# Convolution and expert products of 512 columns in place of 256, in a deformable-convolution, attention and mixture-of-experts kernel

## The chip, the cores and the metric

The kernel runs on one core of a Trainium2 chip. The metric is the device time of one execution in microseconds (us); the median of three executions of the kernel before is 7870.18 us. A core has five engines that this document speaks of: TensorE (PE in the profile; its weight loads are listed apart as PEld), VectorE (DVE), ScalarE (ACT), GpSimd (POOL) and SyncE (SP), the last of which issues most of the DMA transfers here. Each engine runs its instructions in the order in which they were issued to it, and engines wait for each other through semaphores.

## The reference

The input is `x` of shape (4, 128, 64, 64): four images of 128 channels and 4096 positions. Two layers follow each other:

```python
# layer 0
x = x + deform_conv(_gn(x), ...)       # group norm, then a deformable 3x3 convolution
# layer 1, on tokens (4, 4096, 128)
t = _to_tokens(x)
t = t + attn(_ln_t(t), ...)
t = t + experts(_ln_t(t), ...)
```

- The deformable convolution first computes offsets and masks with a 3x3 convolution (27 outputs), gathers four neighbours of each of the nine taps, blends them with bilinear weights times the mask into `samples` (channels x 9 taps x positions), and ends with `einsum('bckhw,ock->bohw', samples, w_flat)`: nine products of a 128x128 weight with the samples of a tap, summed.
- The attention has 16 heads of 8 dimensions over 4096 tokens. Queries, keys and values are the same array, so the score matrix before the softmax is symmetric. A small feed-forward network of 512 hidden units follows.
- The mixture of experts has 8 experts of 128x128. `einsum('bnd,edc->bnec', x, expert_w)` is computed for all eight, the two best by the router are weighted and summed.

All arithmetic is in fp32.

## The kernel before, in words

**The attention loop is the backbone.** For each image, for each of four groups of four heads (`g`) and each chunk of 512 queries (`sc`), a *run* goes through 32 tiles of 128 keys. One tile is one *step*; there are 3700 steps in all. A step has three parts:

- `scores` (line 1147): four fp32r matmuls of 128 keys x 512 queries, one for each head, into two PSUM tiles `sc` of [128, 2, 512], and one exponential over each `sc` tile on ScalarE (line 1164), whose result `e` goes to SBUF. The `sc` tiles come from a pool of three; the `e` tiles from a ring of six.
- the *fill*: at most one piece of other TensorE work, described below.
- `context` (line 1168): four fp32 matmuls that multiply `e` with the values, side by side in four strips of 32 output columns, summed over the run in one PSUM bank `acc`.

The main loop (line 1307) issues the scores of step n+2 (`LAG = 2`), then lets the planner place a fill (line 1335), then issues the context of step n (line 1365). So TensorE's order is: scores of n+2, fill, context of n, scores of n+3, and so on. A fp32 matmul shows in the trace as two records (two passes), an fp32r one as one.

In some runs part of the score matrix is taken from an earlier run by symmetry: VectorE transposes the `e` tiles (`turn`, line 1046), they go to DRAM and come back (`et`), and `from_turned` (line 1096) multiplies them, also as fills.

**All else is done beside it.** Generators produce the other work and yield, ahead of each piece, what it needs of TensorE and VectorE:

- `prepare(b)` (line 762) makes image b ready: group norm, a table of corners in DRAM, offsets (`om_ps`), gathers by GpSimd (line 575), the blend on VectorE (lines 589 to 601), the samples out to DRAM and back as `sT`, and `convolved` (line 633) with the convolution products, then `features`, which yields keys, queries and values. Image 0 is prepared partly ahead of the loop and partly beside its first runs (the *opening*, the first 160 steps), image b+1 during the runs of image b.
- `finish(b, ch)` (line 989) takes a finished chunk of 512 tokens through the output projection (`ao_ps`), the feed-forward network (`h_ps`, `f_ps`) and `experts` (line 882). At the end of the loop what is left is drained.

**The planner `Beside`** (line 62) decides at build time when each piece goes in. It keeps a modelled clock that a step moves on by `STEP = 1.82`, and a TensorE credit that grows by `RATE = 0.44` in a step, is capped at 0.44, and is lowered by a piece's cost `pe`; a piece may start if the credit after it is not under `-LATE = -0.50` (lines 136 and 143). In the opening the growth is 1.0 in a step, with the same cap (line 1299). All fills but those of `from_turned` write to one PSUM bank, `misc` (line 265). A piece that yields `hold=True` locks that bank until its last part has been issued; after that the bank counts as taken until VectorE's modelled read of it ends (lines 122 to 130).

**The two places that the change touches** use `by_columns` (line 270), which issues a product as four matmuls of 32 output columns, one for each strip. In `convolved` (lines 652 to 663) each of the nine taps is two products of 256 columns, `hf` 0 and 1, into the two halves of the bank: 18 pieces for a chunk of 512 positions, 576 in all, with the lock held over all 18. In `experts` (lines 958 to 980), for each of four blocks of 128 tokens and each half of the experts (`hf`), two products of 256 columns (two experts each) fill the bank, and VectorE then reads the 512 columns and multiplies them with the gates (line 970): 16 products of 256 columns for a chunk, 512 in all. Each piece asks for `MM256 = 0.44`, exactly the credit of a step.

Of the kernel before, what the change touches and what calls it, by code (L numbers as in the profile page):

```python
# [22 lines left out]
P = 128  # L23
# [7 lines left out]
KK = 9  # L31
# [162 lines left out]
FREE = -1.0  # L194


def need(pe=0.0, dve=0.0, lat=0.0, hold=False, after=0.0):

    return pe, dve, lat, hold, after


def ve(n, ops=1):

    return ops * (0.17 + n / 960.0)


MM256 = 0.44
MM128 = 0.23  # L210


def tr(n):

    return 0.13 + 0.115 * n
# [3 lines left out]
def kernel(  # L219
# [45 lines left out]
    def misc(name):  # L265
        if alone:
            return ps_s.tile([P, 2, 512], F32, tag="sc", name=name)[:, 0, :]
        return ps_m.tile([P, 512], F32, tag="misc", name=name)

    def by_columns(dst, lhsT, rhs, start, stop):  # L270

        for c in range(0, P, 32):
            nc.tensor.matmul(  # L273
                dst[c : c + 32], lhsT=lhsT[:, c : c + 32], rhs=rhs, start=start, stop=stop
            )
# [7 lines left out]
    def load(ap, shape, name):  # L283
        t = cpool.tile(shape, F32, name=name)
        nc.scalar.dma_start(out=t, in_=ap)
        return t
# [30 lines left out]
    wconv_sb = load(wconv, [P, KK, C], "wconv_sb")  # L317
# [14 lines left out]
    ew_sb = load(ew, [P, NE, C], "ew_sb")  # L332
# [150 lines left out]
    def offsets(b, xn, idx, wt):  # L483
# [3 lines left out]
        for half in range(2):  # L487
# [7 lines left out]
            for n, k in enumerate((4, 0, 1, 2, 3, 5, 6, 7, 8)):  # L495
                for top in range(0, 8, 4):
                    last = n == KK - 1 and top == 4
                    yield need(pe=MM256, dve=ve(512) if last else 0.0, lat=0.2 if last else FREE, hold=not last)
                    if n == 0 and top == 0:
# [63 lines left out]
    def deform(b, tab, idx, wt):  # L563
# [19 lines left out]
        for n, (ch, kg, j) in enumerate(units):  # L583
# [37 lines left out]
            if kg == 2:  # L621

                while featuring:
                    yield need(lat=1.0)
                featuring.append(True)
                beside.later(
                    beside.dve + 0.1,
                    lambda ch=ch: beside.add("prepare", convolved(b, ch), 0.5, True),
                )
# [3 lines left out]
    def convolved(b, ch):  # L633

        xr = work.tile([P, CH], F32, tag="p2", name=f"xr{b}_{ch}", bufs=NP2)
        nc.sync.dma_start(out=xr, in_=xf[b, :, CH * ch : CH * (ch + 1)])
        yield need(lat=2.5)

        sT = big.tile([P, KK, CH], F32, tag="xs", name=f"sT{b}_{ch}")

        def get(kg):
            for c in range(4):
                nc.sync.dma_start(
                    out=sT[32 * c : 32 * (c + 1), 3 * kg : 3 * kg + 3],
                    in_=smd[ch % 2][:, 3 * kg : 3 * kg + 3, c].rearrange("i k o n -> i k (o n)"),
                )

        get(0)
        yield need(lat=6.0)
        get(1)  # L650
        yield need(lat=4.0)
        for k in range(KK):
            if k == 2:
                get(2)
            for hf in range(2):
                last = k == KK - 1 and hf == 1
                yield need(pe=MM256, dve=ve(128, 4) if last else 0.0, lat=0.2 if last else FREE, hold=not last)
                if k == 0 and hf == 0:
                    po = misc(f"conv_ps{b}_{ch}")
                by_columns(  # L660
                    po[:, 256 * hf : 256 * (hf + 1)], wconv_sb[:, k, :],
                    sT[:, k, 256 * hf : 256 * (hf + 1)], k == 0 and hf == 0, last,
                )
        for o in range(4):
            of_block = xr.rearrange("p (j o t) -> p j o t", o=4, t=32)[:, :, o]
            nc.vector.scalar_tensor_tensor(
                of_block, po[:, P * o : P * (o + 1)].rearrange("p (j t) -> p j t", t=32), bconv_sb,
                of_block, ALU.add, ALU.add,
            )
        yield need(pe=tr(4), dve=ve(512))  # L670
        pt = misc(f"x2_ps{b}_{ch}")
        for k in range(4):
            nc.tensor.transpose(pt[:, P * k : P * (k + 1)], xr[:, P * k : P * (k + 1)], ident)
        x2 = work.tile([P, 4, C], F32, tag="p2", name=f"x2_{b}_{ch}", bufs=NP2)
        nc.vector.tensor_copy(x2, pt.rearrange("p (i c) -> p i c", c=C))
        beside.later(beside.dve, lambda: nc.sync.dma_start(out=x2d[b][ch], in_=x2))
        mean = work.tile([P, 4], F32, tag="lt_m", name=f"mean{b}_{ch}")
        rstd = work.tile([P, 4], F32, tag="lt_r", name=f"rstd{b}_{ch}")
        yield from features(b, ch, x2, mean, rstd)
# [107 lines left out]
    def temp2(name, shape=(P, 4, C)):  # L787
        return work.tile(list(shape), F32, tag="f2", name=name, bufs=NF2)
# [93 lines left out]
    def experts(b, ch, x4):  # L882
# [9 lines left out]
        uT = got.pop()  # L892
# [65 lines left out]
        for i in range(4):  # L958
            ws = [temp2(f"eo{b}_{ch}_{i}_{hf}") for hf in range(2)]
            for hf in range(2):  # L960
                for part in range(2):
                    yield need(pe=MM256, dve=ve(512) if part else 0.0, lat=FREE, hold=not part)
                    if part == 0:
                        pe = misc(f"e_ps{b}_{ch}_{i}_{hf}")
                    e0 = 4 * hf + 2 * part
                    by_columns(
                        pe[:, 256 * part : 256 * (part + 1)], uT[:, P * i : P * (i + 1)],
                        ew_sb[:, e0 : e0 + 2, :].rearrange("p e c -> p (e c)"), True, True,
                    )
                nc.vector.tensor_tensor(  # L970
                    ws[hf], pe.rearrange("p (e c) -> p e c", c=C),
                    gt[:, i, 4 * hf : 4 * (hf + 1), None].to_broadcast([P, 4, C]), ALU.mult,
                )
            yield need(dve=ve(512))
            w = ws[0]
            nc.vector.tensor_tensor(w, w, ws[1], ALU.add)
            yield need(dve=ve(256) + ve(128, 2), lat=0.2)
            nc.vector.tensor_tensor(w[:, :2, :], w[:, :2, :], w[:, 2:4, :], ALU.add)
            nc.vector.tensor_tensor(w[:, 0, :], w[:, 0, :], w[:, 1, :], ALU.add)
            nc.vector.tensor_tensor(x4[:, i, :], x4[:, i, :], w[:, 0, :], ALU.add)  # L980
# [8 lines left out]
    def finish(b, ch):  # L989
        x4 = temp2(f"x4_{b}_{ch}")  # L990
        nc.sync.dma_start(out=x4, in_=x2d[b][ch])

        rows = atd[b][ch].rearrange("g (h d) n -> (g h) d n", d=32)
        aT = temp2(f"aT{b}_{ch}", (P, CH))
        nc.sync.dma_start(out=aT, in_=rows[:, :HD])
        rd = work.tile([P, CH // HD], F32, tag="rd", name=f"rd{b}_{ch}")
        nc.sync.dma_start(out=rd, in_=rows[:, HD].rearrange("h (q n) -> h q n", q=HD))
        r = temp2(f"r{b}_{ch}")
        nc.sync.dma_start(out=r, in_=xtd[b][ch])
        yield need(lat=4.0)  # L1000
        yield need(dve=0.6, lat=0.1)
        nc.vector.reciprocal(rd, rd)
        yield need(lat=3.5)
        nc.sync.dma_start(out=rdd[b][ch].rearrange("h q n -> (h q) n"), in_=rd)
        yield need(lat=6.0)
        a4 = temp2(f"a4_{b}_{ch}")
        nc.sync.dma_start(
            out=a4.rearrange("p i c -> p (i c)"),
            in_=rdd[b][ch].rearrange("h q n -> h (q n)")[:, None, :].to_broadcast([HEADS, HD, CH]),
        )  # L1010
        yield from attention_out(b, ch, r, aT, a4)
        yield from feed_forward(b, ch, x4, a4)
        yield from experts(b, ch, x4)
# [82 lines left out]
    def from_turned(run, acc):  # L1096
# [3 lines left out]
        for kt in range(4):  # L1100
# [3 lines left out]
            for half in range(2):  # L1104
                yield need(pe=MM256, hold=None, after=landed)
                for t in (2 * half, 2 * half + 1):
# [135 lines left out]
    for n, (run, t) in enumerate(steps):  # L1242
        b, g, sc = runs[run][:3]
# [56 lines left out]
    with tc.manual_schedule(engines={PE, DVE, SP, POOL}):  # L1300
# [6 lines left out]
        while n < len(steps):  # L1307
# [11 lines left out]
            b, g, sc, ts, kind = runs[run]  # L1319
# [136 lines left out]
```

## Time and profile before

| | |
|---|---|
| median of 3 executions | 7870.18 us (7869.32 to 7878.19) |
| the profiled execution | 7908.98 us, its span 7907.1 us |
| granted TensorE clock, mean | 0.954 |
| PE busy | 7194.3 us (91%) |
| ACT busy | 6874.6 us (87%) |
| DVE busy | 4487.9 us (57%) |
| POOL busy | 1644.6 us (21%) |
| first context matmul begins; what is left after the last run begins | 249.8 us; 7823.7 us |
| `conv_ps` matmuls | 4608 records, 380.7 us busy |
| `e_ps` matmuls | 4096 records (eight groups of 512), 325.2 us busy in sum |

The profiled execution is 0.5% longer than the median. Busy times of TensorE count overlapping strips once, and the ends of its records are modelled; the start times are what to read. ScalarE's records overlap as well: an exponential has a mean record of 1065 ns, but in a stretch without gaps a new one starts every 0.91 us or so, so a step needs 1.82 us of ScalarE. "Idle before" tells how long an engine did nothing before a group of instructions and what ended that.

### The profile page before, as it was taken

To read this page: it belongs to the slowest core of one execution; us is meant where nothing else is said; L and a number is where in the kernel's file an instruction comes from. 1 tells how busy PE (TensorE), PEld (TensorE's weight loads), DVE (VectorE), ACT (ScalarE), POOL (GpSimd) and SP (SyncE) were. 2 spreads that over 40 slices of the span, in tenths; PEclk is the share of its full clock that TensorE was granted. 3 is DMA by queue.
4 is the path that set the end of the run, shared out by engine and by line. 5 is a ranking of instruction groups with operands and counts; after the bars stand their busy time and mean duration, and the time that the engine had idled before them with its cause. 6 is when DMAs were issued, how large, how long until landed. Compare 5 with 4: busy or idle time off the path is not lost.

```text
span 7907.1 us, 182019 instructions
## 1 busy us (share of the span) xinstructions
PE 7194.3 (91%) x73664; PEld 2524.1 (32%) x73664; DVE 4487.9 (57%) x9024; ACT 6874.6 (87%) x7441; POOL 1644.6 (21%) x1326
## 2 busy tenths in 40 slices
PE   2378979999998999999999989989999999999997
PEld 1122222333333333333333333333333333333333
DVE  5666436666453667777554567766444554445434
ACT  0267978988998988989999988888999999999995
POOL 4544114343100332332000133432000000000000
PEclk6688988999999999999999999999999999999998
DMA  6776558888666878898666788988655577877762
GB/s 180 215 214 208 158 150 251 272 260 269 194 190 181 254 228 254 261 293 266 189 187 180 211 278 270 286 282 276 188 175 168 157 234 238 256 240 247 241 212 81
DMA packets 968439, 1757.98 MB, mean 222 GB/s; under 512 B 170864, under 2 KB 436088, under 8 KB 916908
## 3 DMA queue, kind: packets, MB, share of 16 engines
q1 hardware_dynamic: 862590, 1436.61, 60.1%
q0 software_dynamic: 92160, 302.06, 11.9%
q8 instruction: 578, 9.47, 0.5%
q10 hardware_dynamic: 12846, 7.67, 0.4%
q14 instruction: 265, 2.17, 0.1%
HBM read 1063.83 MB, written 682.13 MB: 221 GB/s over the span
## 4 chain that ended last, share of the span: by engine, by line
PE 78%; DMA 8%; DVE 3%; SPq 3%; issue 3%; ACT 3%; POOL 1%; another core or an unknown queue 0%; ACTq 0%; DVEq 0%; POOLq 0%
PE acc L1172 38%; PE sc L1155 23%; PE acc L1108 5%; PE e_ps L273 3%; PE conv_ps L273 3%; ACT e L1164 3%; PE f_ps L273 2%; DMA sT<-smd 2%; DMA et<-etd 1%; DMA kT<-kTd 1%; DMA etd<-st 1%; SPq L476 1%; PE om_ps L507 1%; DMA v<-tab,idx 1%; DVE v L589 1%
## 5 line engine op out<-in xcount | busy, mean ns | idle before, releaser
L1164 ACT ACTIVATE e<-sc 128x1024 f32<-128x1024 f32 x7400 | 6871.5, 1065 | 863.7 <-PE sc L1155 584.6
L1172 PE MATMUL acc<-e,qf 128*32 128x512 f32 x29600 | 3982.3, 608 | 46.1 <-DVE cu L1376 32.9
L1155 PE MATMUL sc<-qT,kT 32*128 32x512 f32 x14800 | 2404.0, 502 | 317.8 <-ACT e L1164 148.2
L1155 PEld LDWEIGHTS sc<-qT,kT 32*128 32x128 f32 x14800 | 960.2, 184 | 3745.1 <-ACT e L1164 3089.6
L575 POOL DMA_INDIRECT v<-tab,idx x1152 | 1444.7, 1254 | 1880.2 <-DVE tr L599 1158.3
L1046 DVE STREAM_TRANSPOSE st<-e 128x1024 f32<-128x1024 f32 x792 | 937.8, 1222 | 833.1 <-ACT e L1164 640.7
L1172 PEld LDWEIGHTS acc<-e,qf 128*32 128x32 f32 x29600 | 804.0, 110 | 614.4 <-issue 339.8
L375 POOL TENSOR_TENSOR r<-ln_t,expo 128x4 f32<-128x4 f32 x96 | 112.3, 1170 | 3151.2 <-DVE ln_t L373 3113.4
L589 DVE TENSOR_TENSOR v<-v,wt 128x1536 f32<-128x1536 f32 x384 | 665.9, 1734 | 103.6 <-DMA v<-tab,idx 78.5
L1108 PE MATMUL acc<-et,qf 128*32 128x128 f32 x12672 | 528.7, 283 | 55.5 <-DMA et<-etd 47.5
L273 PE MATMUL conv_ps<-sT,wconv_sb 128*32 128x256 f32 x4608 | 380.7, 407 | 125.0 <-DMA sT<-smd 121.9
L970 DVE TENSOR_TENSOR eo<-e_ps,gt 128x512 f32<-128x512 f32 x256 | 175.0, 685 | 548.7 <-PE e_ps L273 538.3
L1108 PEld LDWEIGHTS acc<-et,qf 128*32 128x32 f32 x12672 | 305.7, 110 | 259.3 <-issue 191.9
L591 DVE TENSOR_TENSOR v<-v 128x768 f32<-128x768 f32 x384 | 367.3, 957 | 10.7
L1374 DVE COPY cu<-acc 128x512 f32<-128x512 f32 x128 | 88.5, 691 | 442.0 <-PE acc L1172 392.6
L599 DVE STREAM_TRANSPOSE tr<-v 128x128 f32<-128x128 f32 x1152 | 266.0, 282 | 39.0 <-DMA etd<-st 21.1
L592 DVE TENSOR_TENSOR v<-v 128x384 f32<-128x384 f32 x384 | 215.4, 561 | 13.3
L273 PEld LDWEIGHTS conv_ps<-sT,wconv_sb 128*32 128x32 f32 x4608 | 96.9, 110 | 274.6 <-issue 255.1
L375 POOL TENSOR_TENSOR rstd<-lt_t,expo 128x4 f32<-128x4 f32 x32 | 54.3, 1696 | 554.8 <-DVE lt_t L373 554.8
L273 PE MATMUL f_ps<-w_sb,h 128*32 128x128 f32 x4096 | 165.4, 281 | 0.0
L855 DVE TENSOR_SCALAR h<-h_ps,b_sb 128x512 f32<-128x512 f32 x128 | 94.8, 743 | 102.3 <-PE h_ps L853 96.0
L1376 DVE TENSOR_TENSOR cu<-cu,acc 128x512 f32<-128x512 f32 x38 | 26.1, 686 | 207.1 <-PE acc L1172 118.9
(219 smaller groups left out, 3008.8 us busy)
## 6 DMA issues: line engine op xcount, KB each, us to landing
etd<-st SPq DMA_DIRECT2D x1584, 256.0 KB
et<-etd SPq DMA_DIRECT2D x396, 1024.0 KB
kT<-kTd SPq DMA_DIRECT2D x400, 256.0 KB
smd<-tr SPq DMA_DIRECT2D x384, 192.0 KB
sT<-smd SPq DMA_DIRECT2D x384, 192.0 KB
qf<-fqd SPq DMA_DIRECT2D x400, 144.0 KB
qT<-qTd SPq DMA_DIRECT2D x166, 256.0 KB
atd<-cu SPq DMA_DIRECT2D x128, 256.0 KB
```

What stands on the lines that cost most here:

```text
L273: nc.tensor.matmul(dst[c : c + 32], lhsT=lhsT[:, c : c + 32], rhs=rhs, start=start, stop=stop)
L575: nc.gpsimd.indirect_dma_start(out=v[:, k, :], out_offset=None, in_=tab, in_offset=bass.IndirectOffsetOnAxis(ap=idx[:, j, kk : kk + 1], ax ...
L589: nc.vector.tensor_tensor(v4, v4, w12[:, :, None].to_broadcast([P, 12, C]), ALU.mult)
L591: nc.vector.tensor_tensor(v[:, :, : 2 * C], v[:, :, : 2 * C], v[:, :, 2 * C :], ALU.add)
L592: nc.vector.tensor_tensor(v[:, :, :C], v[:, :, :C], v[:, :, C : 2 * C], ALU.add)
L599: nc.vector.transpose(out=tr9[:, k, :, j % 4, :], in_=v[:, k, :C].rearrange("p (c i) -> p c i", i=32),)
L970: nc.vector.tensor_tensor(ws[hf], pe.rearrange("p (e c) -> p e c", c=C), gt[:, i, 4 * hf : 4 * (hf + 1), None].to_broadcast([P, 4, C]), AL ...
L1046: nc.vector.transpose(out=st[:, :, 2 * pr : 2 * pr + 2, :].rearrange("p o h (q j) -> p o (h q) j", j=32), in_=es[pr].rearrange("p h (q o i ...
L1108: nc.tensor.matmul(acc[32 * h : 32 * (h + 1), P * kt : P * (kt + 1)], lhsT=qf[:, t, QW * h : QW * h + 32], rhs=e[:, :, h, 32 * t : 32 * (t ...
L1155: nc.tensor.matmul(ps[i // 2][:, i % 2, :], lhsT=kT[h : h + 32, P * (t % 4) : P * (t % 4 + 1)], rhs=qT[h : h + 32, :], start=True, stop=True,)
L1164: nc.scalar.activation(e, ps[pr], AF.Exp, scale=1.0 / math.sqrt(HD))
L1172: nc.tensor.matmul(acc[32 * h : 32 * (h + 1), :], lhsT=qf[:, t % 4, QW * h : QW * h + 32], rhs=es[h // 2][:, h % 2, :], start=(t == ts[0]) ...
```

## The change

Both places issue one product of 512 columns where they issued two of 256. The number of matmul instructions of these two groups halves, and so does the number of their weight loads; the columns that pass through TensorE are the same. Each piece tells the planner a cost of `MM512 = 0.86` where it told 0.44 twice. In `convolved` the lock is held from tap to tap as before; in `experts` there is no lock any more, since one piece fills the bank. The DVE instructions that read the bank are the same.

```diff
+MM512 = 0.86
 MM256 = 0.44
...
-            for hf in range(2):
-                last = k == KK - 1 and hf == 1
-                yield need(pe=MM256, dve=ve(128, 4) if last else 0.0, lat=0.2 if last else FREE, hold=not last)
-                if k == 0 and hf == 0:
-                    po = misc(f"conv_ps{b}_{ch}")
-                by_columns(
-                    po[:, 256 * hf : 256 * (hf + 1)], wconv_sb[:, k, :],
-                    sT[:, k, 256 * hf : 256 * (hf + 1)], k == 0 and hf == 0, last,
-                )
+            last = k == KK - 1
+            yield need(pe=MM512, dve=ve(128, 4) if last else 0.0, lat=0.2 if last else FREE, hold=not last)
+            if k == 0:
+                po = misc(f"conv_ps{b}_{ch}")
+            by_columns(po, wconv_sb[:, k, :], sT[:, k, :], k == 0, last)
...
-                for part in range(2):
-                    yield need(pe=MM256, dve=ve(512) if part else 0.0, lat=FREE, hold=not part)
-                    if part == 0:
-                        pe = misc(f"e_ps{b}_{ch}_{i}_{hf}")
-                    e0 = 4 * hf + 2 * part
-                    by_columns(
-                        pe[:, 256 * part : 256 * (part + 1)], uT[:, P * i : P * (i + 1)],
-                        ew_sb[:, e0 : e0 + 2, :].rearrange("p e c -> p (e c)"), True, True,
-                    )
+                yield need(pe=MM512, dve=ve(512), lat=FREE)
+                pe = misc(f"e_ps{b}_{ch}_{i}_{hf}")
+                by_columns(
+                    pe, uT[:, P * i : P * (i + 1)],
+                    ew_sb[:, 4 * hf : 4 * hf + 4, :].rearrange("p e c -> p (e c)"), True, True,
+                )
```

Since the planner places pieces by their cost, the order of work changes almost from the first steps on: in the built program of the kernel before, 482 of the 546 steps with a convolution product are followed directly by another such step; in the changed one 188 of 280 have one step without a fill between them and the next.

## The prediction

> **What bounds the kernel now.** I read the page first: busy times, slices, the chain, the costliest groups.
>
> ```profile
> PE 7194.3 (91%) x73664; PEld 2524.1 (32%) x73664; DVE 4487.9 (57%) x9024; ACT 6874.6 (87%) x7441; POOL 1644.6 (21%) x1326
> ...
> ACT  0267978988998988989999988888999999999995
> ...
> PE 78%; DMA 8%; DVE 3%; SPq 3%; issue 3%; ACT 3%; POOL 1%; another core or an unknown queue 0%; ACTq 0%; DVEq 0%; POOLq 0%
> ...
> L1164 ACT ACTIVATE e<-sc 128x1024 f32<-128x1024 f32 x7400 | 6871.5, 1065 | 863.7 <-PE sc L1155 584.6
> ```
>
> TensorE and ScalarE are both nearly full; the chain names TensorE, but ScalarE's exponentials leave little behind it. The windows by stage show both at 99% once nothing is prepared any more, both lower before that:
>
> ```profile
> 2000.00:3000.00 1000.00, 951.64 (x9783) 333.53 (x9784) 538.54 (x1110) 915.30 (x992) 177.66 (x144) 0.97 0.69 208
> ...
> 6000.00:7000.00 1000.00, 994.90 (x10930) 357.26 (x10922) 504.81 (x1154) 993.36 (x1084) 24.51 (x24) 1.00 0.71 213
> ```
>
> (Columns: window, length, busy PE, PEld, DVE, ACT, POOL with counts, clock, DMA share, GB/s.) So what counts is how one step fits. TensorE's timeline, in a stretch of expert products with one empty step:
>
> ```profile
> 7496.43 1.04 PE L1172 MATMUL acc<-e,qf 128*32 128x512 f32 x8
> 7497.40 0.50 PE L1155 MATMUL sc<-qT,kT 32*128 32x512 f32 x4
> 7497.83 0.64 PE L273 MATMUL e_ps<-ew_sb,u_4T 128*32 128x256 f32 x8
> 7498.28 1.04 PE L1172 MATMUL acc<-e,qf 128*32 128x512 f32 x8
> 7499.26 0.50 PE L1155 MATMUL sc<-qT,kT 32*128 32x512 f32 x4
> 7499.69 1.06 PE L1172 MATMUL acc<-e,qf 128*32 128x512 f32 x8
> 7500.68 0.74 PE L1155 MATMUL sc<-qT,kT 32*128 32x512 f32 x4
> 7501.35 0.64 PE L273 MATMUL e_ps<-ew_sb,u_3T 128*32 128x256 f32 x8
> 7501.81 1.04 PE L1172 MATMUL acc<-e,qf 128*32 128x512 f32 x8
> ```
>
> From start to start: scores 0.43, fill of 256 columns 0.46, context 0.97. A filled step is 1.86 (scores 7497.40 to 7499.26), an empty one 1.41 (7499.26 to 7500.68 is 1.42). ScalarE needs 1.82 for a step: in the last row of the next fence five tiles take 4.72, less a record of 1.06 over 4 is 0.91 a tile. After the empty step the scores take 0.67 instead of 0.43: their second pair waits for ScalarE to free the third score tile, and the next filled step lasts 2.13 (context 7499.69 to 7501.81 is 2.12). Over 42 such places the medians are 1.41 and 2.13. An empty step gives TensorE no lasting lead.
>
> What a late score costs shows where a fill came late by itself:
>
> ```profile
> 7576.89 0.50 PE L1155 MATMUL sc<-qT,kT 32*128 32x512 f32 x4
> 7578.35 1.04 PE L1172 MATMUL acc<-e,qf 128*32 128x512 f32 x8
> 7579.32 0.50 PE L1155 MATMUL sc<-qT,kT 32*128 32x512 f32 x4
> ...
> 7579.92 4.72 ACT L1164 ACTIVATE e<-sc 128x1024 f32<-128x1024 f32 x5 [0.46 <-PE sc L1155]
> ```
>
> Scores to context took 1.46 instead of 0.43, 1.03 more than an empty step; ScalarE took up the scores 0.60 after their start and had stood idle for 0.46. So a fill up to 1.03 - 0.46 = 0.57 passes unseen by ScalarE, and what is above that is lost.
>
> **The change, part by part.**
>
> *Fewer matmuls.* 2304 of 4608 conv records and 2048 of 4096 expert records go, with as many weight loads. TensorE's price of a wide product: in a context group, which has the same strips and 512 columns, the two passes start 0.43 apart (single records of the trace), so 2 x 0.43, and with the 0.03 that the 256-column product has over its own two passes about 0.88; bounds 0.86 and 0.97 (the context with its change to row strips). Two narrow ones are 0.92. That saves 0.04 a pair, 544 x 0.04 = 22 us if TensorE alone set the pace; it is contained in the steps below. The Trainium skill, page "TensorEngine Tiling (Array Packing)", section "Instruction Overhead", gives each matmul some 60 cycles of overhead; at the 2.4 GHz of the page "TensorE: Matmul & The Clock Gate" that would be, as an estimate, 4352 x 25 ns = 109 us off TensorE's time, five times what the rows allow.
>
> *Where the wide fills stand.* The credit allows a 0.86 piece every second step. In the built program of the changed kernel 279 wide conv and 248 wide expert products stand in the loop; 36 of the conv ones stand in the opening's first 160 steps, at one a step, and the other 491 have at least one step without such a product between (empty in 188 conv and 96 expert cases; further apart for most of the rest). A step with a wide fill needs 0.43 + 0.88 + 0.97 = 2.28 of TensorE, 0.46 more than ScalarE's 1.82. By the idle row, 0.88 is 0.31 over the 0.57 that passes. The scores queue behind the wide fill on TensorE, and ScalarE waits for them. The second of those pages (Part 2, "What happens when you issue a matmul") says that matmuls stay in program order, which speaks against this change since the next scores can't pass a longer fill; in the timeline above, indeed, no score row begins ahead of the context row before it.
>
> *Price of a pair.* Before: two filled steps, 2 x 1.865 = 3.73. After: an empty step 1.41, and a filled one that follows it, 2.13 + (0.88 - 0.46) = 2.55: together 3.96. That is 0.23 a wide product; the other way, 0.31 of idle ScalarE less the 2 x 0.04 that narrow steps already lose to 1.82, also gives 0.23. Clean steps, 1.80 to 1.92 long in the trace of before, were 358 of 541 conv steps and 370 of 484 expert steps; I apply those shares. Clean: 243 x 0.66 + 248 x 0.76 = 349, x 0.23 = 80 us. In the other 142 the step was already held up by VectorE or DMA (conv steps of 3 us and more, 119 of them, where ScalarE or the turned tiles are late), and a wide fill hides in part: between 0 and 0.31 each, 0 to 44 us; I take half the clean price, 16 us.
>
> *The bank.* Before, VectorE's read (0.69) of an expert bank lies between two consecutive steps; after, there are two steps for it. Gains at most the few us that TensorE now waits for `eo` (3.5 in the listing of that tile). VectorE's read, issued right behind the fill, waits up to 0.42 longer, with the turning transposes behind it: 256 x 0.42 = 108 us of VectorE idle at worst, covered by its 43% idle time; without that cover the turned tiles are late next. I take 0, and keep part of it in the upper range.
>
> *The opening.* The last chunk of image 0 is ready at step 292 instead of 279. If preparing sets the pace there (the first 200 steps average 2.84 us, 203 us over 1.82 each), 13 more steps pass in its shadow, -24 us; if not, the longer opening costs as much. The chain there is mixed; I take -10. Its wide products, at one a step, take 2.28 for what took two steps of 1.86, and the empty step so gained is ScalarE's to use: within the same bounds. The transfers of SyncE and the gathers of GpSimd are the same ones, some at other steps; images 1 to 3 are ready within 20 steps of where they were, and I take 0 for that.
>
> *The end.* Before, three expert pairs and the last transposes of chunk 6 remain after the loop; after, they are done inside it. VectorE works on them from 7824.7 to 7835.6, but chunk 7's inputs land only around 7830 (its last load issues at 7828.6): 5 us gained (0 to 11). Chunk 7's own expert products are paced by VectorE there: 0.
>
> Sum: 80 + 16 + 0 - 10 - 5 = 81 us on the profiled execution's 7908.98, which lies 0.5% over the median. Scaled to the median, 7870 x 81/7909 = 81: **7951 us**, 1.0% slower.
>
> **The rivals.**
>
> *Absorbed (faster).* The three score tiles and six `e` tiles absorb the late scores, TensorE alone sets the pace, and a pair costs 2.28 + 1.41 = 3.69 instead of 3.73: 491 x -0.04 = -20, with -10 and -5 about 7835. For it: transposes of 0.59 pass unseen (steps 2.00, 1.43, 1.67). Against it: the 0.46 row. It decides if a fill of 0.88 leaves ScalarE idle for less than 0.08.
>
> *Slow wake.* Some of ScalarE's late starts come 0.87 after the scores, not 0.60 (scores at 3006.49, exponential at 3007.36). If most wide fills meet that, 349 x 0.27 = 94 us more: 8045. Against it: starts with idle of 0.1 to 0.3 are nearly all at 0.60.
>
> *Covered (same).* The loop's other stalls hide most of the clean cases too, and the opening gains its 24 us: 81 - 60 - 14 = +7, 7877. Against it: from about 5600 us on nothing is prepared any more, both engines run at 99% with no stall to hide in, and over half of the expert products stand there.
>
> **How the numbers follow.** Forecast 0.72, its own range 7895 to 8010 (the held-up steps at 0 or 0.31, opening +24 or -24, part of VectorE's waiting); absorbed 0.13; slow wake 0.09; covered 0.06. The range 7850 to 8040 leaves out the absorbed case and about half of the slow wake. Within 0.2% (16 us, about what this measurement can tell from no change): 0.06; faster 0.13; slower 0.81.
>
> **What would show it.** Right: wide steps of about 2.5 us after empty ones and ScalarE idle for 0.3 before the next scores; `sc` as ScalarE's releaser up from 584.6 by some 80 to 150 us; the window from 6000 to 7000 no longer at 99% on ACT; conv and expert records halved with TensorE's busy time lower. Wrong: ACT still without gaps around wide fills; an opening that ends tens of us earlier or later; VectorE's `st` transposes late behind `eo`.

## The result, and the profile after

The changed kernel takes 7968.74 us (median of four, 7967.02 to 7983.08) against 7869.75 us before (7863.6 to 7878.19). The ratio is 1.0127, with a 95% interval of 1.0114 to 1.0139: 1.3% slower, 99 us. The forecast was 7951.

The profiled execution of the changed kernel spans 7965.2 us. The lines of its page that answer to those shown of before (the lines of the file have moved: `scores` is L1149 and L1158, `context` L1166, `by_columns` L274):

```profile
PE 7283.8 (91%) x69312; PEld 2443.2 (31%) x69312; DVE 4491.2 (56%) x9024; ACT 6901.8 (87%) x7441; POOL 1649.3 (21%) x1326
...
PE 79%; DMA 7%; DVE 4%; SPq 3%; issue 3%; ACT 2%; POOL 0%; another core or an unknown queue 0%; ACTq 0%; POOLq 0%; DVEq 0%
...
L1158 ACT ACTIVATE e<-sc 128x1024 f32<-128x1024 f32 x7400 | 6898.8, 1063 | 901.2 <-PE sc L1149 606.3
...
L274 PE MATMUL conv_ps<-sT,wconv_sb 128*32 128x512 f32 x2304 | 325.4, 641 | 125.3 <-DMA sT<-smd 120.5
```

TensorE has 4352 matmul records fewer, and the convolution's busy time falls from 380.7 to 325.4 us; still the sum of TensorE's busy time rises. ScalarE's idle time has grown too, from 863.7 to 901.2 us, but what it waited for the scores only from 584.6 to 606.3. The page says little of what was lost; the windows say where:

```profile
2000.00:3000.00 1000.00, 950.84 (x9308) 323.16 (x9304) 547.64 (x1140) 913.91 (x988) 168.18 (x137) 0.97 0.68 204
6000.00:7000.00 1000.00, 998.07 (x10373) 349.05 (x10369) 519.11 (x1222) 985.59 (x1072) 27.84 (x27) 1.00 0.69 208
```

In the late window ScalarE starts 1072 exponentials where it started 1084: with two for a step, 1.1% less of the work in the same time. Busy shares hide this nearly (993 against 986), because the records overlap by some 0.14 us: an idle time under that is not seen as idle. The count is the better reading.

The timeline of TensorE and ScalarE, in a stretch of expert products:

```profile
7411.19 5.67 ACT L1158 ACTIVATE e<-sc 128x1024 f32<-128x1024 f32 x6
...
7412.39 0.51 PE L1149 MATMUL sc<-qT,kT 32*128 32x512 f32 x4
7412.82 1.07 PE L1166 MATMUL acc<-e,qf 128*32 128x512 f32 x8
7413.82 0.84 PE L1149 MATMUL sc<-qT,kT 32*128 32x512 f32 x4
7414.59 1.06 PE L274 MATMUL e_ps<-ew_sb,u_3T 128*32 128x512 f32 x8
7415.47 1.04 PE L1166 MATMUL acc<-e,qf 128*32 128x512 f32 x8
7416.44 0.50 PE L1149 MATMUL sc<-qT,kT 32*128 32x512 f32 x4
7416.88 1.06 PE L1166 MATMUL acc<-e,qf 128*32 128x512 f32 x8
7417.04 3.77 ACT L1158 ACTIVATE e<-sc 128x1024 f32<-128x1024 f32 x4 [0.19 <-PE sc L1149]
7417.87 0.74 PE L1149 MATMUL sc<-qT,kT 32*128 32x512 f32 x4
7418.54 1.06 PE L274 MATMUL e_ps<-ew_sb,u_3T 128*32 128x512 f32 x8
```

The wide fill takes 0.88 (7414.59 to 7415.47). The scores behind it start at 7416.44, 2.62 after the ones before, and ScalarE takes them up 0.60 later, having stood idle. The listing gives 0.19 of idleness; from start to start of two exponentials the median behind a wide expert product is 1.23 us, 0.33 more than the 0.905 without a gap. After the empty step that follows (scores 7416.44 to 7417.87, 1.43), the second pair of scores has to wait for a score tile again (0.67 from scores to fill, not 0.43). Over the whole trace an empty step and the wide one after it take 3.97 us in the median, where two narrow ones took 3.73.

### The profile page after: what moved, and what is told of

The parts are those of the page before. It is cut to its first block, busy times and chain, and to the rows that moved or that the text cites. A ratio compares the mean times of both kernels' runs of the same rounds, so it can differ in the third digit from the quotient of the medians.

```text
span 7965.2 us, 173309 instructions
## 1 busy us (share of the span) xinstructions
PE 7283.8 (91%) x69312; PEld 2443.2 (31%) x69312; DVE 4491.2 (56%) x9024; ACT 6901.8 (87%) x7441; POOL 1649.3 (21%) x1326
## 3 DMA queue, kind: packets, MB, share of 16 engines
q14 instruction: 265, 2.17, 0.1%
## 4 chain that ended last, share of the span: by engine, by line
PE 79%; DMA 7%; DVE 4%; SPq 3%; issue 3%; ACT 2%; POOL 0%; another core or an unknown queue 0%; ACTq 0%; POOLq 0%; DVEq 0%
PE acc L1166 39%; PE sc L1149 23%; PE acc L1102 5%; PE conv_ps L274 3%; PE e_ps L274 3%; ACT e L1158 2%; DMA sT<-smd 2%; PE f_ps L274 2%; DMA et<-etd 1%; DVE v L590 1%; SPq L477 1%; PE om_ps L508 1%; SPq L613 1%; DMA qT<-qTd 1%; SPq L752 0%
## 5 line engine op out<-in xcount | busy, mean ns | idle before, releaser
L1158 ACT ACTIVATE e<-sc 128x1024 f32<-128x1024 f32 x7400 | 6898.8, 1063 | 901.2 <-PE sc L1149 606.3
L1166 PE MATMUL acc<-e,qf 128*32 128x512 f32 x29600 | 4013.0, 611 | 40.4 <-DVE cu L1370 20.4
L1149 PE MATMUL sc<-qT,kT 32*128 32x512 f32 x14800 | 2477.4, 501 | 252.2 <-ACT e L1158 128.6
L1149 PEld LDWEIGHTS sc<-qT,kT 32*128 32x128 f32 x14800 | 1020.1, 184 | 3702.9 <-ACT e L1158 2824.0
L1166 PEld LDWEIGHTS acc<-e,qf 128*32 128x32 f32 x29600 | 758.9, 110 | 883.5 <-issue 781.0
L274 PE MATMUL conv_ps<-sT,wconv_sb 128*32 128x512 f32 x2304 | 325.4, 641 | 125.3 <-DMA sT<-smd 120.5
L274 PE MATMUL f_ps<-w_sb,h 128*32 128x128 f32 x4096 | 165.6, 281 | 0.0
L728 POOL COPY fx<-rn 128x512 f32<-128x512 f32 x32 | 31.5, 986 | 618.7 <-DVE rn L727 360.7
```

The costliest lines, as they stand in the source:

```text
L274: nc.tensor.matmul(dst[c : c + 32], lhsT=lhsT[:, c : c + 32], rhs=rhs, start=start, stop=stop)
L1149: nc.tensor.matmul(ps[i // 2][:, i % 2, :], lhsT=kT[h : h + 32, P * (t % 4) : P * (t % 4 + 1)], rhs=qT[h : h + 32, :], start=True, stop=True,)
L1158: nc.scalar.activation(e, ps[pr], AF.Exp, scale=1.0 / math.sqrt(HD))
L1166: nc.tensor.matmul(acc[32 * h : 32 * (h + 1), :], lhsT=qf[:, t % 4, QW * h : QW * h + 32], rhs=es[h // 2][:, h % 2, :], start=(t == ts[0]) ...
```

## The experiments

All later runs were on other chips, on which the kernel before takes 7732 to 7737 us instead of 7870. Each run's ratio is to runs of the kernel before on its own chip. Times by stage come from one profiled execution each and are held against one profile of the kernel before, taken on another of these chips; executions of the kernel before spread over 25 us, so a difference of some 10 us by stage is not clear of noise. These times are taken from the starts of the context matmuls: steps 0 to 300 (the opening and what remains of image 0), 300 to 2500 (runs beside which images are prepared), 2500 to the last context, and the end.

### The kernel before, once more

No edit.

> The kernel before, unchanged, profiled a second time. The first profile of it was 7908.98 us, 39 over its median, and its first 160 steps took 485.5 us against 433.8 in the changed kernel. If that was one slow opening, this profile spans about 7870 and the opening about 445, and the rest keeps its times (steps 2500 to 3400 in 1671.5 us). Rival: the opening takes 485 again, so the change really gains some 50 us there and loses some 150 later.

7723.9 us, its span 7722.0. The opening's 160 steps took 463.5 us, not 485.5, and steps 2500 to 3400 the same 1671.5 as in the first profile. So the opening of the first profile was slow by this measure, but on another chip; that the changed kernel has the shorter opening stands (425.7 in its run below). The other 150 us of the first profile over this run lie in steps 300 to 2500 (4557 against 4406 us). The first chip's trace lists waits there that this one doesn't: 46 us of ScalarE for "remote" (another core or a queue unknown to the profile), 15 us of ScalarE and 44 of TensorE for "issue". They are less than the 150; why the first chip was slower there is not settled. The further comparisons by stage use this profile.

### The changed kernel on such a chip

> The changed kernel again, beside the kernel before on the chip of this call. The piece of two joined products took 0.888 from its start to the next context and the wide one 0.882, so by the theory the joined and the wide kernel are within 491 x 0.006 = 3 us: if the chip behaves as in the last call (before at 7736), this gives about 7882, +1.9%. Rival (the wide instruction is itself better than two joined ones by some 50 us, 1.27% against 1.94%): 7835.

7882.29 us, ratio 1.019 (1.017 to 1.021), as expected from the joined products below. The loss on these chips is 150 us, not 99.

| stage, us | before | changed | wide experts alone | wide convolution, images 1 to 3 | joined narrow products |
|---|---|---|---|---|---|
| steps 0 to 300 | 759.0 | 738.4 | 755.5 | 753.6 | 736.5 |
| 300 to 2500 | 4405.5 | 4561.7 | 4466.8 | 4499.2 | 4551.4 |
| 2500 to the last | 2228.1 | 2263.4 | 2269.7 | 2231.2 | 2263.9 |
| the end | 83.7 | 78.9 | 78.7 | 79.1 | 78.9 |
| median of the run | 7732 to 7737 | 7882 | 7824 | 7829 | 7885 |

### Half of the change: the experts alone

Convolution in 256 columns, experts as in the change's diff.

> Wide expert products alone, convolution in 256 columns. Theory (a wide fill is 0.31 us over what passes unseen by ScalarE, 0.23 us a pair in clean steps, half in held-up ones): 248 x (0.76 x 0.23 + 0.24 x 0.115) = 50, the end -5: 7915 us. Rival (the loss is in the stretches that prepare an image, from late turned tiles and the convolution): the experts cost 0.23 only after the last preparation, some 33 us, the rest nothing: 7895 us.

7823.79 us, ratio 1.0111 (1.0093 to 1.0129): 87 us slower, where I expected 45 and the rival 25. The late stage lost 41.6 us. Of the 248 wide expert products in the loop, 98% leave a gap of 0.25 us or more on ScalarE, 0.33 in the median; of narrow ones 2% do. The step behind the expectation that fell is the half price for held-up steps: there is hardly a wide product without its gap, wherever it stands. The other part, 61 us in the preparing stage, is more than its wide products can cost (104 of 0.33 us), and is taken up below.

### The other half: the convolution of images 1 to 3

```diff
+            if b >= 1:
+                last = k == KK - 1
+                yield need(pe=MM512, dve=ve(128, 4) if last else 0.0, lat=0.2 if last else FREE, hold=not last)
+                if k == 0:
+                    po = misc(f"conv_ps{b}_{ch}")
+                by_columns(po, wconv_sb[:, k, :], sT[:, k, :], k == 0, last)
+                continue
             for hf in range(2):
```

> Wide convolution products for images 1 to 3 alone; image 0, so the whole opening, and the experts as before. Theory by the recorded terms: 216 x (0.66 x 0.23 + 0.34 x 0.115) = 41 us, +0.5%. If held-up steps hide nothing, 216 x 0.32 less what the narrow ones lost (0.06) = 56 us. Rival (the convolution is covered by the stalls of the preparing stages): under 15 us. Steps from 2500 on unchanged at 2228 us.

7829.33 us, ratio 1.013 (1.011 to 1.015): 97 us slower, more than any of the theories said. The late stage, without convolution, is as before (+3). In the preparing stage it lost 94 us, the experts alone 61, and the whole change 156: the two halves add up. With the wide convolution in the opening left out, 15 of the 21 us gained there are gone too (753.6 against 738.4). The wide convolution in the opening alone was not tried, so this stands as the difference of two columns of the table, and a new order alone could gain as much (18 us, with a modelled step of 1.80, below).

### Width or length: joined narrow products

The planner's pieces and costs of the changed kernel, each piece two products of 256 columns one behind the other:

```diff
-            by_columns(po, wconv_sb[:, k, :], sT[:, k, :], k == 0, last)
+            for hf in range(2):
+                by_columns(
+                    po[:, 256 * hf : 256 * (hf + 1)], wconv_sb[:, k, :],
+                    sT[:, k, 256 * hf : 256 * (hf + 1)], k == 0 and hf == 0, last and hf == 1,
+                )
...
-                by_columns(
-                    pe, uT[:, P * i : P * (i + 1)],
-                    ew_sb[:, 4 * hf : 4 * hf + 4, :].rearrange("p e c -> p (e c)"), True, True,
-                )
+                for part in range(2):
+                    e0 = 4 * hf + 2 * part
+                    by_columns(
+                        pe[:, 256 * part : 256 * (part + 1)], uT[:, P * i : P * (i + 1)],
+                        ew_sb[:, e0 : e0 + 2, :].rearrange("p e c -> p (e c)"), True, True,
+                    )
```

> The pieces and the planner's costs of the changed kernel, so its order of work, but each piece issues two products of 256 columns one behind the other. Theory (the loss comes from the length of a piece and from its place, not from the width of an instruction): a piece takes 0.92 instead of 0.88, 491 x 0.04 = 20 us more than the changed kernel: 7989 us, steps with a pair after an empty step 2.60. Rival (matmuls of 512 columns are what costs): back at 7870 to 7900.

7884.74 us, ratio 1.0194 (1.0177 to 1.0211): the same as the changed kernel on such chips (7882.29, 1.019). The timeline of its TensorE:

```profile
7256.41 0.75 PE L1155 MATMUL sc<-qT,kT 32*128 32x512 f32 x4
7257.10 1.07 PE L274 MATMUL e_ps<-ew_sb,u_2T 128*32 128x256 f32 x16
7257.98 1.04 PE L1172 MATMUL acc<-e,qf 128*32 128x512 f32 x8
```

Two narrow products behind each other take 0.88 (the median of single starts is 0.888, of a wide one 0.882). So the instruction's width is worth 0.006 us, 3 us in all. As far as these two ratios can tell (0.2% each), the whole loss belongs to the length of the piece and to its place, and none of it to the 512 columns of an instruction. My 20 us more was wrong: the 0.03 that a narrow product has over its own two passes is not paid a second time when two follow each other.

### A dose between: 384 and 128 columns

```diff
-                yield need(pe=MM256, dve=ve(128, 4) if last else 0.0, lat=0.2 if last else FREE, hold=not last)
+                yield need(pe=MM128 if hf else MM384, dve=ve(128, 4) if last else 0.0, lat=0.2 if last else FREE, hold=not last)
...
-                    yield need(pe=MM256, dve=ve(512) if part else 0.0, lat=FREE, hold=not part)
+                    yield need(pe=MM128 if part else MM384, dve=ve(512) if part else 0.0, lat=FREE, hold=not part)
```

with the columns cut at 384, and `MM384 = 0.65`.

> Each pair is split into 384 and 128 columns instead of 256 and 256, the planner told 0.65 and 0.23. Theory: a fill of 384 columns takes about 0.67, 0.10 over the 0.57 that passes; two steps cost 3.64 + 0.10 = 3.74, as the two narrow ones before (3.73): 7870 us, within 20; ScalarE's gaps behind the wide piece 0.1. Rival (any piece over the credit of a step costs in proportion to its columns over 256): half of the change's loss, 7920 us.

7720.61 us, ratio 0.9981 (0.9969 to 0.9992): within 0.2% of before, and on its lower side. A fill of 384 columns takes 0.67, and ScalarE's gap behind it is 0.13 (1.04 from start to start). With 0.03 for 0.46 and 0.33 for 0.88, the gap grows with the length of the fill above some 0.5 us, and the pair costs in the late stage 20 us more than before (2248.4), for about as many pairs as lost 35 to 42 us with wide fills. That is more than the nothing I expected; the opening (748.0, 11 less), the preparing stage (4398.4, 7 less) and the end (4 less) made up for it, by amounts that are hardly clear of noise. The rival's half loss did not come.

### Taking the cause away: a slower ScalarE

If ScalarE's supply is the cause, the loss must go when ScalarE needs more time for a step, though TensorE does the same. A first pair added an exponential that did not depend on the score tile:

```diff
+    dump = cpool.tile([P, 96], F32, name="dump")
...
             nc.scalar.activation(e, ps[pr], AF.Exp, scale=1.0 / math.sqrt(HD))
+            nc.scalar.activation(dump, ident[:, :96], AF.Exp)
```

> The kernel before with a further small exponential on ScalarE (128x96, result not used) behind each exponential of a score tile, so that ScalarE and not TensorE has to be waited for. With some 0.2 us more for each tile a step needs 2.2 us of ScalarE: 3700 x 0.4 = 1400 us more, less what was stalls, about 8900 to 9100 us. Steps of 2.2 with a 256-column fill and without; ScalarE without gaps.

> The changed kernel with the same small exponential. Theory: with a tile of a us ScalarE starves behind a fill longer than 3a - 2.17 (0.55 at 0.905, 1.13 at 1.1), so a wide fill of 0.88 passes unseen; ScalarE's gaps behind wide fills vanish and this kernel is within 30 us of the slowed kernel before (opening and end gain some 25). Rival (the loss lies in TensorE's time, in the order of the work or in late turned tiles, not in ScalarE's narrow supply): still 100 to 150 us slower than the slowed kernel before.

9406.6 and 9519.16 us, 113 apart: by its number that is what the rival said. But the pair is no test of it. ScalarE's order is not written out by hand, and the added exponentials ran ahead of their place: at 1000 us 1486 of them had begun in the slowed kernel before, against 491 of the score tiles. The last one began at 5432 us (5540 in the changed kernel), so the late stage was as in the kernels without them (2231.5 and 2263.7 us).

The second pair ties the added exponential to the score tile, which also is freed later:

```diff
+            nc.scalar.activation(dump, ps[pr][:, 1, :96], AF.Exp)
```

> The kernel before with the small extra exponential reading the score tile itself, so that it stays behind its own exponential and the tile is freed later (in the first slowed pair the extra ones ran ahead of their place). One took 0.31 us there: a tile takes about 1.22, a step 2.44; 3700 x 2.44 and the rest, about 9400 us; narrow fills leave no gap on ScalarE, nor do empty steps.

> The changed kernel with the same. Theory (the loss is ScalarE running dry behind a fill longer than 3a - 2.17, which is 1.49 at a = 1.22): no gaps behind wide fills, steps from 2500 on as in the slowed kernel before within 5 us, the whole within 30 us, rather faster (opening -20, end -5). Rival (TensorE's own time or later transfers carry the loss): 35 us slower from step 2500 on, 100 us and more in all.

8550.61 and 8588.29 us: 38 apart instead of 150, where I expected 30 at most. The added exponential costs less than I thought: a tile takes 1.035 us, a step 2.07. By the rule of 3a - 2.17 (three score tiles of a us each; the 2.17 makes it 0.55 at 0.905) a fill of 0.93 then passes, just over the wide fill's 0.88. It does not quite: over 1.035, the median gap is still 0.09 us behind a wide convolution product and 0.14 behind a wide expert product, instead of 0.33. The rule gives the direction and not the size. ScalarE in the two kernels' late stages, first the slowed kernel before, then the slowed changed one (columns as in the windows above):

```profile
5918.00:8462.00 2544.00, 2481.55 (x24916) 950.89 (x24911) 1058.53 (x2451) 2541.61 (x4812) 53.33 (x52) 1.00 0.61 184
```

```profile
5955.00:8505.00 2550.00, 2478.33 (x23742) 888.10 (x23741) 1064.32 (x2447) 2542.21 (x4812) 51.31 (x50) 1.00 0.60 183
```

The late loss falls from 35 us to 6 (I had said 5 at most), and both opening and end gain (803.7 to 773.8, 84.1 to 79.9). The same windows without the added exponential, before and changed:

```profile
5410.00:7638.00 2228.00, 2217.32 (x24914) 805.59 (x24906) 1055.14 (x2451) 2215.16 (x2415) 53.35 (x52) 1.00 0.68 210
```

```profile
5546.00:7810.00 2264.00, 2254.37 (x23746) 792.81 (x23744) 1062.58 (x2447) 2224.20 (x2416) 51.92 (x51) 1.00 0.67 206
```

Here the same 2415 exponentials stretch over 36 us more. With ScalarE the slower engine, the same TensorE work costs 6. ScalarE's gaps count up to the same: from start to start over 0.905, those under 0.7 us, about twice the gap behind a wide fill, add up to 49 us in the late stage before and 86 in the changed kernel, 37 more; in the slowed pair, over 1.035, to 60 and 61. That settles the late stage. But in steps 300 to 2500 the slowed changed kernel still lost 70 us (4863.8 to 4933.9). There the same gaps grew by 20 us only, so they are not the main reason.

### What a change of order costs

The kernel before with nothing but another modelled step for the planner (`STEP = 1.82`), so that the same narrow pieces stand at slightly other places and the transfers come in another order.

```diff
-    STEP = 1.82
+    STEP = 1.84
```

> The kernel before with the planner's modelled step at 1.84 instead of 1.82: the same pieces of 256 columns, slightly other places, other order of transfers. It shows what a change of order alone does. Theory: within 25 us of the kernel before, either way, with the steps from 2500 on within 10 us of 2228. Rival (most of the loss in the preparing stages is the change of order as such): 50 us and more slower.

```diff
-    STEP = 1.82
+    STEP = 1.80
```

> The same with a modelled step of 1.80. Theory: within 25 us of the kernel before, either way. Rival: 50 us and more slower.

7770.05 us (ratio 1.0037, 1.0024 to 1.005) and 7760.02 us (1.0026, 1.0017 to 1.0036): 33 and 23 us slower in all, the first above the 25 that I expected, the second within, both under the rival's 50. But by stage: 56 and 65 us lost in steps 300 to 2500 (4461.5 and 4470.8), about as much as in the slowed pair; 7 and 4 us gained in the late stage; the end 5 us shorter, as in the changed kernel. So a new order alone can lose about 60 us in the preparing stage. It need not: the kernel of 384 and 128 columns has another order too, with other pieces, and lost nothing there. What TensorE and ScalarE wait for in that stage, first in the kernel before:

```profile
PE acc L1108 <- DMA et<-etd: 71.1, 21, 14.9
PE conv_ps L273 <- DMA sT<-smd: 9.3, 2, 8.3
```

```profile
ACT e L1164 <- PE sc L1155: 147.6, 52, 17.8
```

and in the changed kernel:

```profile
PE acc L1102 <- DMA et<-etd: 110.0, 22, 19.2
PE conv_ps L274 <- DMA sT<-smd: 52.1, 10, 10.6
```

```profile
ACT e L1158 <- PE sc L1149: 288.8, 304, 20.8
```

(Waiting instruction, what it waited for, us in total, times, longest.) Two losses are seen side by side. ScalarE waits for scores 304 times instead of 52: these are the gaps, many and short. And TensorE waits 82 us longer for the turned score tiles and the samples: late transfers, few and long. The second kind is there in the slowed pair too (turned tiles 19.1 and 68.8 us, between 2000 and 6000 us).

The second kind has a companion. The same stage in the two kernels as a window (the third number from the end is the granted TensorE clock):

```profile
1004.00:5410.00 4406.00, 4176.03 (x43147) 1451.43 (x43147) 2793.50 (x5319) 4083.37 (x4420) 1185.49 (x955) 0.98 0.80 247
```

```profile
985.00:5546.00 4561.00, 4285.08 (x40719) 1425.63 (x40719) 2808.93 (x5364) 4103.73 (x4419) 1201.10 (x958) 0.96 0.78 240
```

In the traces the granted clock is either 1 or 0.5 of full speed, and it is 0.5 in this stage for 167 us before and for 338 us in the changed kernel. All 22 stretches of more than 3 us in which TensorE stood still there in the changed kernel had a half clock in them or within 7 us behind them. An example from the changed kernel, behind a late load of samples:

```profile
4637.17 1.93 PE L274 MATMUL conv_ps<-sT,wconv_sb 128*32 128x512 f32 x8 [9.01 <-DMA sT<-smd]
4638.88 1.93 PE L1166 MATMUL acc<-e,qf 128*32 128x512 f32 x8
4640.74 0.80 PE L1149 MATMUL sc<-qT,kT 32*128 32x512 f32 x4
4641.47 1.85 PE L1166 MATMUL acc<-e,qf 128*32 128x512 f32 x8
```

The wide product takes 1.71 us here instead of 0.88, the context 1.86 instead of 0.97. So this late transfer cost its wait and then slow steps.

Steps 300 to 2500 of every kernel, in us. The gaps are ScalarE's, from start to start of its exponentials, over 0.905 (1.035 in the slowed pair); with 4400 times that they add up to the time of the stage.

| kernel | time | gaps under 0.7 | longer gaps | clock at 0.5 |
|---|---|---|---|---|
| before | 4406 | 89 | 335 | 167 |
| changed | 4562 | 162 | 418 | 338 |
| joined narrow products | 4551 | 157 | 413 | 307 |
| wide experts alone | 4467 | 114 | 372 | 198 |
| wide convolution, images 1 to 3 | 4499 | 128 | 390 | 246 |
| 384 and 128 columns | 4398 | 110 | 307 | 184 |
| modelled step 1.84 | 4462 | 92 | 388 | 242 |
| modelled step 1.80 | 4471 | 85 | 404 | 225 |
| slowed, before | 4864 | 92 | 218 | 133 |
| slowed, changed | 4934 | 112 | 268 | 276 |
| first chip, before | 4557 | 102 | 473 | 242 |
| first chip, changed | 4641 | 170 | 490 | 314 |

The short gaps follow the width of the fills: they grow by 73 us with all fills wide, by 25 and 39 with each half, by 67 on the first chip, and not with a new order. The long gaps go with the order: they grow by 53 and 70 with the order alone, by 84 in the changed kernel, and shrink with 384 columns. This is a sorting by size and no full proof: many of the kernel before's gaps of 1.0 to 1.5 us stand behind its convolution products, and move when the products do, so another limit than 0.7 gives other shares. And in the kernel with wide experts alone the long gaps grew by 37 us while the waits for turned tiles and samples grew by 4: what makes them there stays open.

## Why the prediction was right, and where it was not

**The direction and the size.** 7951 forecast, 7968.74 measured; +81 against +99. On the other chips it was +150, just above the likeliest case's own range (+25 to +140 over 7870) and within the whole range (up to +170). That own range was wider than its terms: the ones that I listed give 7921 at the low end, and nothing on record leads down to 7895. On the first chip the parts agree too: ScalarE's gaps under 0.7 us grew by 67 us in the preparing stage and by 37 in the late one, 104 against the 96 that I had for wide fills; longer gaps in the preparing stage added 17; the end gave 5 back. That is 116; the other 17 us were gained elsewhere, 4 in longer gaps of the late stage and, by estimate, 13 ahead of step 300, if what the first profile had over its median lay in its slow opening.

**"TensorE's price of a wide product ... about 0.88."** 0.882. Two narrow ones take 2 x 0.456 = 0.91 in two steps and 0.888 joined, so of the 0.03 saved nearly all comes from standing together and not from width. The estimate from the Trainium skill's page TensorEngine Tiling (Array Packing), section Instruction Overhead, 109 us off TensorE's time, is not borne out: 4352 matmul records fewer gave 2 us between joined and wide (7884.74 and 7882.29, each uncertain by some 13).

**"Price of a pair", 3.73 to 3.96.** Right in the median, by the word: 2.55 for the wide step after an empty one (2.557 measured), 1.41 for the empty one, and a gap of 0.33 on ScalarE for the 0.31 that I took.

**"A fill up to 0.57 passes unseen".** Right only with luck. I read the threshold from the idle column (0.46), which does not see the first 0.14 us or so; from start to start ScalarE had lost 0.60 there. And that row followed filled steps, with nothing in store for ScalarE, whereas a wide fill follows an empty one. The two errors seem to have cancelled. The doses of 0.46, 0.67 and 0.88 show gaps of 0.03, 0.13 and 0.33.

**"In the other 142 the step was already held up ... a wide fill hides in part".** This step failed: the half price was too low, and its 16 us too small. 96% of the wide convolution products and 99% of the wide expert products leave a gap of 0.25 us or more on the second chip (92 and 99% on the first). At the full price for all, 491 x 0.23 is 113 us, and the gaps under 0.7 us grew by 104 on the first chip and 110 on the second. My reading, which no run isolates, is that a step that has waited for VectorE or DMA does not refund the scores that come late behind a long fill, since ScalarE ends such a wait empty as well.

**"Images 1 to 3 are ready within 20 steps of where they were, and I take 0 for that."** On the chips of the experiments this is the larger miss: the longer gaps of steps 300 to 2500 grew by 84 us, where a changed order alone made 53 and 70, with late turned tiles and samples and TensorE at half clock for twice as long. No row of one profile could have given it; the two kernels with another modelled step did. On the first chip the term was nearly right: longer gaps of 473 us before and 490 after, so that of the 84 us lost in the stage 67 are short gaps. Its kernel before was already slow there (4557 us, not 4406); whether another order would cost less on that chip was not tried.

**"The opening, I take -10"; "the end, 5 us gained".** The opening with what follows gained 21 us on the second chip, near the full shadow of 24; a new order alone gained 0 or 18, so the shadow is not shown to be its reason. The end gained 4.8 us.

**Sum by the runs, second chip:** late stage +35 (gaps), preparing stage +156 (73 in gaps under 0.7 us, 84 in longer ones), opening -21, end -5: 165 between the profiles, 167 with what lies ahead of the first context; they stand 8 below and 8 above the medians of that chip, and 150 lie between medians.

**The rivals.** *Absorbed*: no; it needed a gap under 0.08. *Slow wake*: no; the median gap is 0.33, not 0.6, and the exponential starts 0.60 after the scores in the median. *Covered*: no; the stage with the stalls lost the most.

**The signs.** Of those for being right, the wide steps of 2.5 us, the gaps of 0.3 and the halved records came, and ACT in the window from 6000 to 7000 fell just under 99% (985.59 us). Two did not: `sc` as ScalarE's releaser rose by 22 us, not by 80 to 150, since the idle column misses the first 0.14 us of every gap and sums many other waits; and TensorE's busy time rose from 7194.3 to 7283.8 us. Of those for being wrong, the opening did end tens of us earlier (433.8 against 485.5 us for its 160 steps, 425.7 against 463.5 on the other chips).

## What to carry to other kernels

When two engines are both nearly full and one feeds the other through a shallow buffer, work it out step by step: a filler must fit the slack of a single step, and the same sum of work in pieces of twice the length, every second step, starves the consumer although the sums still fit. Here a limit estimated from one timeline and held against a filler's length told the direction and nearly the size, though the limit came out right with luck. Where a planner places the work, the effect of a new order is a term of its own, and is sized by kernels, more than one, that change the order and nothing else. And read the granted clock by stage: here a late transfer was paid a second time in slow steps.

## What was not expected of the hardware

- Two products of 256 columns that follow each other directly take 0.888 us, one of 512 columns 0.882: at this size twice the number of matmul instructions cost 0.006 us.
- An exponential of 128x96 placed behind one of 128x1024 added only 0.13 us to the 0.905 from start to start, although its own record lasts 0.28 us in the median of the first slowed pair, and 0.87 and 0.68 us in the medians of the second.
- The kernel before took 7870 us on one chip and 7732 to 7737 us on others; steps 2500 to 3400 took 1671.5 us on both. Of the 185 us between the two profiles 151 lie in steps 300 to 2500, beside which images are prepared, and 31 ahead of them.
- TensorE's granted clock was at half in or right behind all 22 standstills of more than 3 us in steps 300 to 2500 of the changed kernel, and behind one of them a 512-column product took 1.71 us instead of 0.88.
